# Feed-forward pieces that end with their sums: residual and second norm moved into the next token stage

## The chip, the cores and the metric

One core of a Trainium2 chip runs the whole program. A core has TensorE (PE, matmuls; its weight loads are shown apart as PEld), VectorE (DVE), ScalarE (ACT), GpSimd (POOL) and SyncE (SP), which here only issues transfers. The five run side by side. Each takes its own instructions in the order in which the program names them, and waits in front of one whose inputs or buffers are not ready. The metric is the device time of one execution in microseconds; the median of the runs stands for a kernel.

## What is computed

Four images of 64 x 64 positions and 256 channels, all in float32. A first layer adds the output of full attention over the 4096 positions. The second is triangle attention over rows with a feed-forward part and two layer norms:

```python
f, g, v = xt @ Wf + bf, xt @ Wg + bg, xt @ Wh + bh
beta = softmax(einsum('bqd,bkd->bqk', g, f))
x = x + (einsum('bqk,bkd->bqd', beta, v) @ Wo0 + bo)

q, k, v1, v2 = x @ Wq, x @ Wk, x @ Wv1, x @ Wv2          # 8 heads of 32
att = softmax(einsum('bilhd,bljhd->biljh', q, k) / sqrt(32), axis=2)
out = einsum('biljh,bilhd,bljhd->bijhd', att, v1, v2)
h = layer_norm(x + out @ Wo1) * ln_agg_g + ln_agg_b
mlp = relu(h @ W1 + b1) @ W2 + b2
return layer_norm(mlp + h) * ln_out_g + ln_out_b
```

## The kernel before

The order of all instructions is written by hand: what the Python code emits first stands first in its engine's queue. The batches go one after the other, and each has two stages.

**The token stage** (`layer0`) is the first layer. It walks through 64 groups g, eight to a query block of 512 (k = g % 8). In `values(g)` PE multiplies the exponents of group g with the values (L571) and makes the scores of group g + 1 in between (L544); ACT turns them into exponents (L556), in two halves of 1024 columns; DVE adds them up (L578). Scores have two buffers of two banks (tag "a"), exponents two (tag "k8"). From the second query block on, the eight groups also carry parts of the block before: at k = 0 the denominator (L596), its reciprocal, the product and two reductions on DVE (L600, L602, L610), at k = 1 the output (L623, and L624 on DVE), then the projections. The first query block has none of these parts.

**The triangle stage** (`first_layer1` for batch 0, `next_layer1` for the others) has 32 steps. It goes by a list of words, run through once per period of two steps; a word `R14/2` is product 4 of the period's second step, two periods late. R multiplies attention weights with v2 on DVE or POOL (L999), A accumulates the product on PE (L1009), T copies the sum out on ACT (L1019) and the second T stores it with eight transfers, S and W make weights, t and c turn them, V prepares wsel, sp and sf make scores and e and f take them. Products on DVE share three buffers (R), those on POOL two (Rp). Scores are made in 11 of the periods after the first.

Batch 1's triangle stage also carries the feed-forward of batch 0, batch 2's that of batch 1, and batch 3's that of batch 2 and the first pieces of its own. One piece of 256 positions goes with each period: h0 and h1 make x + attention output in PSUM (hps), sa takes its mean and variance, rr and pp make the scale and shift from them (Ln and Exp on ACT, seven small instructions on POOL), fa normalises into `h` (one buffer), ht turns it on PE, hT makes the input of the hidden layer from that, and hU, in `carried`, a second turned copy with the residual's scale and bias. m, r and z are the two feed-forward layers; z also turns hU's copy back into the sums in PSUM with four transposes (L1240). so takes the sums' mean and variance on ACT, and rr and pp handle them together with those of the next piece's first norm. fo normalises, and fi either finishes the piece (batch 3) or sends z off to a DRAM tile `raw` (`put_off`).

These pieces come back in the next token stage: at g = 3t `recall` fetches piece t, at g = 3t + 2 `finish` scales and shifts it on POOL (L1248, L1249) and writes it out. All of these transfers, the stores of the projections and those of the triangle stage go through SP's queue, in order.

The places that the change and the steps of the prediction touch: the list `ORDER` (L43), the calls of `recall` and `finish` in `layer0` (L752 to L755), `rest.carried` at its end (L816), `put_off` and `recall` (L1045 to L1054), `stats`, `sums_of`, `roots`, `polish`, `affine`, `carried`, `outputs` and `finish` (L1090 to L1250), and the words sa, so, rr, pp, fo, hU and fi in `next_layer1`.

Of the kernel before, what the change touches and what calls it, by code (L numbers as in the profile page):

```python
# [10 lines left out]
F32 = mybir.dt.float32  # L11
# [4 lines left out]
ALU = mybir.AluOpType  # L16
AX = mybir.AxisListType

P = 128
C = 256  # L20
# [9 lines left out]
NP = T // 256  # L30
# [10 lines left out]


ORDER = """  # L43
    r0/1 A10/2 A11/2 m1/1 R14/2 R05/1 S1/1 R15/2 T10/2 sp/1 A14/2 A16/2 r1/1 e0/1 e1/1 A15/2 A05/1 T11/2 R04/1
    A04/1 z0/1 W1/1 R03/1 V1/1 fi/2 S0 z1/1 t1/1 so/1 R06/1 R00/1 c1/1 sa A03/1 R07/1 R02/1 A06/1 A02/1 A00/1
    rr/1 pp/1 W0 R01/1 A07/1 A01/1 fo/1 fa T01/1 R12/1 t0 T00/1 R17/1 h1/-1 sf/1 R13/1 h0/-1 f0/1 ht f1/1 R16/1
# [20 lines left out]
def attention_then_triangle_kernel(  # L67
# [6 lines left out]
    nc = tc.nc  # L74
    NB = x.shape[0]
# [5 lines left out]
    work = ctx.enter_context(tc.tile_pool(name="work", bufs=2))  # L81
# [29 lines left out]
    back_t = ctile([P, 4], "back")  # L111
# [50 lines left out]
    lag_bc = brow(lag, C, "lag_bc")  # L162
# [327 lines left out]
    def layer0(b, F, safe, rest, ahead):  # L490
# [238 lines left out]
        for g in range(8 * NQB):  # L729
            qb, k = divmod(g, 8)  # L730
            if b == 0 and not safe:
                for load in later[3 * g : 3 * g + 3]:
                    load()
                if g == 6:
                    fold_bias()
                if g == 20:
                    add_b2()
            if safe and k == 0 and qb + 1 < NQB:
                mx, todo = pieces(qb + 1)
                for qc, t in todo:  # L740
                    max_piece(qc, t, mx)
                row[qb + 1] = max_row(mx)
            values(g, g + 1 < 8 * NQB)

            if qb > 0 and not (qb == last and k >= 6 + late):
                for part in parts[k]:
                    part(qb - 1)
            if late and g % 2 == 0 and 0 <= g // 2 - 2 < ahead.n:
                ahead.bring(g // 2 - 2)
            if late and g % 2 == 1 and 0 <= g // 2 - 3 < ahead.n:  # L750
                ahead.turn(g // 2 - 3)
            if b > 1 and g % 3 == 0 and g < 3 * NP:  # L752
                rest.recall(NP * (b - 2) + g // 3)
            if b > 1 and g % 3 == 2 and g < 3 * NP:
                rest.finish(NP * (b - 2) + g // 3)  # L755
            if qb == last and k == 3:
                L.fetch_v1(0)
                L.fetch_v1(1)
            if qb == last and k == 5:
                if b > 0:  # L760
                    rest.load(NP * (b - 1))
                L.fetch_qk(0, True)
# [49 lines left out]
        if old:  # L812
            rest.turn(t0)
            rest.load(t0 + 1)
            rest.normed(t0)
            rest.carried(t0)  # L816
        if not late:
            values1(1)
        score(2)
# [216 lines left out]
    class Tokens:  # L1036
        def __init__(self):
            self.ios = []
            self.A, self.htp = {}, {}
            self.h, self.hT, self.hT2, self.hid, self.z, self.zp, self.hps = {}, {}, {}, {}, {}, {}, {}  # L1040
            self.mv = self.rs = None
            self.raw = {}


        def put_off(self, tt):  # L1045
            b, t = divmod(tt, NP)
            if t == 0:
                self.raw[b] = dram.tile([NP, P, 2, C], F32, tag="raw", name="raw")
            nc.sync.dma_start(out=self.raw[b][t], in_=self.z.pop(tt))

        def recall(self, tt):
            b, t = divmod(tt, NP)
            self.z[tt] = work.tile([P, 2, C], F32, tag="s4", name="z")
            nc.sync.dma_start(out=self.z[tt], in_=self.raw[b][t])  # L1054

        def load(self, tt, far=False):
            b, t = divmod(tt, NP)
# [332 lines left out]
    def words_of(order):  # L1390
        for w in order:
            w, late = (w.split("/") + ["0"])[:2]
            yield w, int(late)
# [58 lines left out]
    def next_layer1(b, L, rest, ahead, F):  # L1452
        own = b == NB - 1
        t0 = NP * (b - 1)


        n2, n1, n0 = NP, NP + own, NP + 2 * own
        stored, held = set(), []
        mv, rs, rn, mps = {}, {}, {}, {}

        def fetched(step):
            if F is not None and 24 <= step < 31:
                ahead.fetch(F, b + 1, step)


        def load(q, far=False):
            if q < NP or 24 + (q - NP) // 2 in stored:
                rest.load(t0 + q, far)
            else:
                held.append((q, far))  # L1470

        def was_stored(step):
            stored.add(step)
            if own and step == 26:
                held.extend((NP + q, True) for q in (2, 3, 4))
            todo, held[:] = list(held), []
            for q, far in todo:
                load(q, far)

        def moments(q):  # L1480
            if q not in mv:
                mv[q] = small.tile([P, 4, 2], F32, tag="mv", name="mv")
            rest.mv = mv[q]

        def of_piece(word, q):
            tt = t0 + q
            first, second = 1 <= q < n1, 0 <= q < n2
            if word in ("h0", "h1"):
                if 2 <= q < n0:
                    n = int(word[1])  # L1490
                    rest.heads(tt, n, new=q not in mps)
                    mps.setdefault(q, {})["h", n] = True
                    if len(mps[q]) == 2 and q + 1 < n0:
                        load(q + 1)
            elif word == "sa" and first:
                moments(q - 1)
                rest.stats(rest.hps[t0 + q], 0)
            elif word == "so" and second:
                moments(q)
                z = rest.z[t0 + q] = work.tile([P, 2, C], F32, tag="s4", name="z")  # L1500
                rest.sums_of(rest.zp[t0 + q], z, rest.mv, 2)
            elif word == "rr" and second:
                moments(q)
                rest.roots(0 if q + 1 < n1 else 2, 4)
                rs[q] = rest.rs
            elif word == "pp" and second:
                moments(q)
                rest.rs = rs.pop(q)
                rest.polish(0 if q + 1 < n1 else 2, 4, nc.gpsimd, back=back_t)
                rn[q] = rest.rn  # L1510
            elif word == "fa" and first:
                rest.rn = rn[q - 1]
                rest.affine_a(tt)
            elif word == "fo" and second:
                rest.rn = rn[q]
                rest.affine_o(tt)
            elif word == "ht" and first:
                rest.turn(tt)
            elif word == "hT" and first:
                rest.normed(tt)  # L1520
            elif word == "hU" and first:
                rest.carried(tt)
            elif word in ("m0", "m1") and first:
                n = int(word[1])
                mps[q][n] = [rest.hidden(tt, fc) for fc in (2 * n, 2 * n + 1)]
            elif word in ("r0", "r1") and first:
                n = int(word[1])
                for fc, mp in zip((2 * n, 2 * n + 1), mps[q][n]):
                    rest.rectify(tt, fc, mp)
            elif word in ("z0", "z1") and second:  # L1530
                n = int(word[1])
                rest.outputs(tt, n, new=tt not in rest.zp)
                mps.setdefault(q, {})["z", n] = True
            elif word == "fi" and second:
                (rest.finish if own else rest.put_off)(tt)

        def spread(step):
            if F is not None:
                ahead.spread(F, b + 1, step)

        step_word, scores, take_scores = step_words(L, fetched, was_stored, spread)
        mps[1] = {}
        for period in range(NP + 4):
            for word, late in words_of(ORDER):
                i = period - late
                if i == 0 and word in ("A05", "A04"):
                    for m in (4, 5) if word == "A04" else ():
                        step_word("A", 0, m)
                elif word[0] in "RATSWVtc":
                    step_word(word[0], 2 * i + int(word[1]), int(word[-1]))  # L1550
                elif word in ("sp", "sf"):
                    if (i == 0) == (word == "sf"):
                        scores(i)
                elif word in ("e0", "e1", "f0", "f1"):
                    if (i == 0) == (word[0] == "f"):
                        take_scores(i, int(word[1]))
                else:
                    of_piece(word, i)
        assert not held
        if F is not None:  # L1560
            ahead.fetch(F, b + 1, NSTEP)
# [68 lines left out]
```

## Time and profile before

| | us |
|---|---|
| median of 3 runs | 3650.46 (3650.37 to 3651.98) |
| the profiled execution | 3654.27 |
| its span, first to last instruction | 3652.5 |
| token stage of batch 1 (872.4 to 1257.8) | 385.4 |
| token stages of batches 2 and 3 | 385.7, 385.6 |
| batch 1's triangle stage, first sums to the next stage's scores (1295.9 to 1744.4) | 448.5 |

Busy time of each engine over the span:

```profile
PE 3544.0 (97%) x22410; PEld 1909.6 (52%) x22410; DVE 2739.5 (75%) x2326; ACT 1934.8 (53%) x4209; POOL 1805.7 (49%) x918
```

The groups of instructions that the change touches or that its cost is taken from; the columns are busy time and mean ns of one, then the idle time of the engine before them and what ended it:

```profile
L1186 ACT ACTIVATE hT<-htp,lab_sb,lag_sb 128x256 f32<-128x256 f32 x226 | 109.6, 563 | 24.2 <-PE htp L1181 24.2
L1097 DVE BATCH_NORM_STATS2 st<-hp 128x6 f32<-128x256 f32 x128 | 52.8, 412 | 17.6 <-PE hp L1086 17.6
L1158 ACT ACTIVATE z<-zp,rn 128x256 f32<-128x256 f32 x98 | 50.0, 561 | 33.2 <-POOL rn L1153 31.5
L1098 DVE BATCH_NORM_AGGREGATE mv<-st 128x2 f32<-128x6 f32 x160 | 29.1, 182 | 8.6 <-DVE st L1097 0.5
L1124 ACT ACTIVATE ln<-mv,eps 128x4 f32<-128x4 f32 (+2 forms) x83 | 25.7, 309 | 64.4 <-DVE mv L1098 60.4 <-issue 3.5 <-DVE nt L1136 0.5
```

An engine that is idle costs nothing by itself; what counts in each stage is the one that the others wait for.

### The profile page before, as it was taken

How to read it: one execution, taken by the hardware profiler on the slowest of the kernel's cores; microseconds unless marked ns; L12 is line 12 of the kernel's file. 1: busy time of each engine (PE TensorE's matmuls, PEld its weight loads, DVE VectorE, ACT ScalarE, POOL GpSimd, SP SyncE). 2: the span in 40 equal slices, each digit the busy share in tenths (PEclk: the TensorE clock that was granted, in tenths of full speed). 3: DMA queues.
4: the chain of work that ended last, by engine and by line, in shares of the span. 5: the costliest groups of instructions: out<-in, count | busy, mean ns of one | idle time of the engine just before them, and what ended most of it. 6: DMA issues, size and time to landing. Idle time of an engine off the chain costs nothing.

```text
span 3652.5 us, 58549 instructions
## 1 busy us (share of the span) xinstructions
PE 3544.0 (97%) x22410; PEld 1909.6 (52%) x22410; DVE 2739.5 (75%) x2326; ACT 1934.8 (53%) x4209; POOL 1805.7 (49%) x918
## 2 busy tenths in 40 slices
PE   9999899988999999999999999999999999999998
PEld 6555444434555555554455555554455555555477
DVE  4777599996555479999565549999755556999976
ACT  3444455544444367666444457676544436777654
POOL 5000199994000068889311028889722106999910
PEclk9999999999999999999999999999999999999999
DMA  9544555465111343425422153333522225341221
GB/s 174 140 130 121 137 150 143 118 135 126 52 49 52 97 116 95 94 51 104 101 80 79 58 144 92 78 89 66 129 73 78 75 83 137 91 96 47 68 69 52
DMA packets 487987, 353.38 MB, mean 97 GB/s; under 512 B 302673, under 2 KB 433489, under 8 KB 478865
## 3 DMA queue, kind: packets, MB, share of 16 engines
q1 hardware_dynamic: 438656, 322.58, 33.1%
q0 software_dynamic: 36160, 19.94, 5.1%
q10 hardware_dynamic: 12880, 7.01, 0.7%
q8 instruction: 179, 2.93, 0.3%
q14 instruction: 112, 0.91, 0.1%
HBM read 197.34 MB, written 152.04 MB: 96 GB/s over the span
## 4 chain that ended last, share of the span: by engine, by line
PE 68%; POOL 5%; DVE 4%; issue 3%; ACT 2%; DMA 1%; SPq 0%; ACTq 0%; DVEq 0%; POOLq 0%
PE o L571 18%; PE acc L1009 15%; PE proj L638 6%; PE mp L1214 6%; PE zp L1234 5%; PE s L544 5%; POOL Rp L999 4%; DVE R L999 3%; PE sp L897 3%; PE hp L1081 3%; PE v1p L670 2%; PE y L623 1%; PE att L951 1%; PE htp L1181 1%; PE hp L1086 1%
## 5 line engine op out<-in xcount | busy, mean ns | idle before, releaser
L999 POOL TENSOR_TENSOR Rp<-attP,v 128x2048 f32<-128x2048 f32 x328 | 1491.1, 4576 | 463.3 <-ACT attP L959 367.8
L999 DVE TENSOR_TENSOR R<-att,v 128x2048 f32<-128x2048 f32 x696 | 1547.7, 2274 | 67.7 <-PE acc L1009 49.4
L571 PE MATMUL o<-e,v 128*128 128x512 f32 x2048 | 1043.6, 592 | 0.0
L578 DVE TENSOR_TENSOR esum<-esum,e 128x2048 f32<-128x2048 f32 x224 | 525.0, 2344 | 508.9 <-ACT e L556 505.6
L556 ACT ACTIVATE e<-s 128x1024 f32<-128x1024 f32 x512 | 523.4, 1024 | 581.3 <-PE s L544 484.6
L544 PE MATMUL s<-gT,fT 128*128 128x512 f32 x1024 | 785.6, 769 | 8.6 <-ACT e L556 5.1
L1009 PE MATMUL acc<-R,wsel 128*32 128x512 f32 x5568 | 705.7, 602 | 37.2 <-DVE R L999 29.4
L571 PEld LDWEIGHTS o<-e,v 128*128 128x128 f32 x2048 | 388.7, 190 | 275.9 <-issue 233.6
L1009 PE MATMUL acc<-Rp,wsel 128*32 128x512 f32 x2624 | 344.3, 596 | 11.1 <-POOL Rp L999 10.4
L1019 ACT COPY ao<-acc 128x1024 f32<-128x1024 f32 x256 | 254.4, 1021 | 189.6 <-PE acc L1009 153.1
L1009 PEld LDWEIGHTS acc<-R,wsel 128*32 128x32 f32 x5568 | 152.1, 109 | 384.5 <-issue 277.9
L544 PEld LDWEIGHTS s<-gT,fT 128*128 128x128 f32 x1024 | 194.2, 190 | 243.9 <-issue 231.0
L1142 POOL TENSOR_SCALAR nt<-mv 128x4 f32<-128x4 f32 (+1 forms) x51 | 9.8, 192 | 627.2 <-DVE mv L1098 623.1
L1248 POOL TENSOR_TENSOR z<-z,log_bc 128x512 f32<-128x512 f32 x48 | 71.8, 1496 | 452.2 <-DMA z<-raw 434.5
L934 ACT ACTIVATE es<-S,rd 128x64 f32<-128x64 f32 x1024 | 257.8, 336 | 16.6 <-DVE rd L926 13.8
L1214 PE MATMUL mp<-hT,w 128*128 128x256 f32 x1024 | 249.5, 389 | 0.7 <-ACT hT L1186 0.7
L1234 PE MATMUL zp<-w,hid 128*128 128x256 f32 x1024 | 245.0, 385 | 0.8 <-ACT hid L1223 0.8
L1214 PEld LDWEIGHTS mp<-hT,w 128*128 128x128 f32 x1024 | 186.8, 190 | 101.2 <-ACT attP L959 36.0
L1234 PEld LDWEIGHTS zp<-w,hid 128*128 128x128 f32 x1024 | 185.7, 190 | 62.3 <-issue 29.3
L600 DVE RECIPROCAL rec<-den 128x512 f32<-128x512 f32 x32 | 107.4, 3358 | 119.4 <-PE den L596 114.0
L1009 PEld LDWEIGHTS acc<-Rp,wsel 128*32 128x32 f32 x2624 | 81.5, 110 | 197.8 <-issue 139.0
L1223 ACT ACTIVATE hid<-mp,b_sb 128x256 f32<-128x256 f32 x256 | 105.2, 469 | 117.7 <-PE mp L1214 117.7
(180 smaller groups left out, 3665.7 us busy)
## 6 DMA issues: line engine op xcount, KB each, us to landing
v<-v2d SPq DMA_DIRECT2D x44, 512.0 KB
v1c<-v1d SPq DMA_DIRECT2D x128, 128.0 KB
aT<-ao SPq DMA_DIRECT2D x1024, 16.0 KB
A<-aT SPq DMA_DIRECT2D x256, 64.0 KB
out_dram<-z SPq DMA_DIRECT2D x63, 256.0 KB
y<-yT SPq DMA_DIRECT2D x56, 256.0 KB
q<-st SPq DMA_DIRECT2D x56, 256.0 KB
k<-st SPq DMA_DIRECT2D x52, 256.0 KB
```

The lines of the kernel that those rows point to most:

```text
L544: nc.tensor.matmul(s_ps[r // 2][:, r % 2, :], fT[tt][:, ts(r * 4 + n, P)], gT[qb // 4][:, ts(qb % 4, QB)], start=True, stop=not safe,)
L556: nc.scalar.activation(e[g][:, 2 * j : 2 * j + 2, :], s_ps[j], AF.Exp)
L571: nc.tensor.matmul(o_ps[qb], F.v[tt][:, r * 4 + n, :], es[:, r, :], start=(k == 0 and r == 0), stop=(k == 7 and r == 3),)
L578: nc.vector.tensor_tensor(esum[qb], esum[qb], es, ALU.add)
L638: nc.tensor.matmul(ps, w[:, cc, rows], y(qb, cc), start=(cc == 0), stop=(cc == 1))
L897: nc.tensor.matmul(sp[ts(h, 64), lh, n, :], k[rows, u * 8 + n, :], q[rows, u * 8 + n, :], start=True, stop=True,)
L934: nc.scalar.mul(e[:, i, :], rows[:, i, :], rec[:, i : i + 1])
L999: eng.tensor_tensor(R, src.unsqueeze(1).to_broadcast([P, D, N]), v2[h], ALU.mult)
L1009: nc.tensor.matmul(acc[32 * c : 32 * c + 32, n % 2, :], w[:, n, c, 16 * h : 16 * h + 32], R[:, ts(c, 8), :].rearrange("p d j -> p (d j)"), ...
L1019: nc.scalar.copy(self.ao[step][:, ts(np, 2)].rearrange("p k d j -> p k (d j)"), self.acc[step][np])
L1214: nc.tensor.matmul(self.mp[:, fc % 2, :], w1_sb[:, cc, ts(fc, P)], self.hT[tt][:, cc, :], start=(cc == 0), stop=(cc == 1),)
L1234: nc.tensor.matmul(zp[:, n, :], self.hid[tt][:, fc, ts(n, P)], w2_sb[:, fc, :], start=(fc == 0), stop=(fc == 3 and tt not in self.hT2),)
```

## The change

For batches 0 and 1 (the pieces that go with the triangle stages of batches 1 and 2) the piece ends with the sums of the second feed-forward layer. so becomes a plain copy out of PSUM, fi sends that copy off, and hU sends off `h` as fa left it, with no second turned copy and so without the four transposes back. rr and pp handle the first norm alone, and sa takes its sums on ACT (`sums_of`) where DVE took them. The DRAM tile `raw` holds both halves of a piece, 0.5 MB.

In the next token stage `recall` fetches both into a tile of tag R. At g = 3t + 2 `settle` makes the residual on DVE (h times its scale, plus its bias, added to z), takes the statistics on DVE and Ln and Exp of them on ACT. At g = 3t + 3, ahead of the next `recall`, `conclude` does the small instructions of the norm on DVE, the two normalising activations on ACT and `finish` on POOL. Batch 3's triangle stage keeps the old order as `ORDER_LAST`; the two others go by a new list.

```diff
 ORDER = """
+    R17/2 A10/2 A12/2 R13/2 fo/2 f1/2 ht/1 h1 hT/1 t0/1 m0/1 A13/2 R14/2 A11/2 R15/2 R02/1 f0/2 R16/2 W1/1 c0/1
+    A17/2 r0/1 T10/2 A14/2 R05/1 A16/2 V0/1 A15/2 sp/1 T11/2 R03/1 m1/1 h0 t1/1 A02/1 e0/1 R01/1 e1/1 S0 c1/1
+    r1/1 sa A03/1 A05/1 fi/2 V1/1 R07/1 R00/1 R06/1 S1 A01/1 z1/1 W0 R04/1 rr/1 z0/1 hU/1 R10/1 A00/1 A07/1
+    A06/1 pp/1 R12/1 T00/1 A04/1 so/1 fa T01/1 sf/1 R11/1
+""".split()
+ORDER_LAST = """
...
+            if b > 1 and g % 3 == 0 and 0 < g <= 3 * NP:
+                rest.conclude(NP * (b - 2) + g // 3 - 1)
             if b > 1 and g % 3 == 0 and g < 3 * NP:
                 rest.recall(NP * (b - 2) + g // 3)
             if b > 1 and g % 3 == 2 and g < 3 * NP:
-                rest.finish(NP * (b - 2) + g // 3)
+                rest.settle(NP * (b - 2) + g // 3)
...
-            rest.carried(t0)
+            (rest.carried if b == NB - 1 else rest.carried_off)(t0)
...
+        def carried_off(self, tt):
+            self.put_off(tt, 0, self.h.pop(tt))
+
+        def summed_off(self, tt):
+            self.put_off(tt, 1, self.z.pop(tt))
 
         def recall(self, tt):
             b, t = divmod(tt, NP)
-            self.z[tt] = work.tile([P, 2, C], F32, tag="s4", name="z")
-            nc.sync.dma_start(out=self.z[tt], in_=self.raw[b][t])
+            self.both[tt] = work.tile([P, 2, 2, C], F32, tag="R", name="hz", bufs=3)
+            nc.sync.dma_start(out=self.both[tt], in_=self.raw[b][t])
+
+        def settle(self, tt):
+            both = self.both.pop(tt)
+            h, z = both[:, 0], both[:, 1]
+            nc.vector.tensor_tensor(h, h, lag_bc.unsqueeze(1).to_broadcast([P, 2, C]), ALU.mult)
+            nc.vector.tensor_tensor(h, h, lb2_bc.unsqueeze(1).to_broadcast([P, 2, C]), ALU.add)
+            nc.vector.tensor_tensor(z, z, h, ALU.add)
+            self.z[tt] = z
+            self.stats(z, 2)
+            self.roots(2, 4)
+            self.settled[tt] = self.mv, self.rs
+            self.mv = None
+
+        def conclude(self, tt):
+            self.mv, self.rs = self.settled.pop(tt)
+            self.polish(2, 4, nc.vector)
+            self.affine(self.z[tt], self.z[tt], 2)
+            self.finish(tt)
...
             elif word == "sa" and first:
                 moments(q - 1)
-                rest.stats(rest.hps[t0 + q], 0)
+                if own:
+                    rest.stats(rest.hps[tt], 0)
+                else:
+                    junk = work.tile([P, 2, C], F32, tag="sx", name="junk", bufs=1)
+                    rest.sums_of(rest.hps[tt], junk, rest.mv, 0)
             elif word == "so" and second:
+                z = rest.z[tt] = work.tile([P, 2, C], F32, tag="s4", name="z")
+                if own:
+                    moments(q)
+                    rest.sums_of(rest.zp[tt], z, rest.mv, 2)
+                else:
+                    nc.scalar.copy(z, rest.zp.pop(tt))
...
-            elif word == "fo" and second:
+            elif word == "fo" and second and own:
...
-                rest.carried(tt)
+                (rest.carried if own else rest.carried_off)(tt)
...
-                (rest.finish if own else rest.put_off)(tt)
+                (rest.finish if own else rest.summed_off)(tt)
```

More of the change, by code (lines that the diff above doesn't have):

```diff
@@ L1041, in __init__, with put_off @@
             self.mv = self.rs = None
-            self.raw = {}
-        def put_off(self, tt):
+            self.raw, self.both, self.settled = {}, {}, {}
+        def put_off(self, tt, part, src):
             b, t = divmod(tt, NP)
-            if t == 0:
-                self.raw[b] = dram.tile([NP, P, 2, C], F32, tag="raw", name="raw")
-            nc.sync.dma_start(out=self.raw[b][t], in_=self.z.pop(tt))
+            if b not in self.raw:
+                self.raw[b] = dram.tile([NP, P, 2, 2, C], F32, tag="raw", name="raw")
+            nc.sync.dma_start(out=self.raw[b][t][:, part], in_=src)
+        def carried_off(self, tt):
+            self.put_off(tt, 0, self.h.pop(tt))
+        def summed_off(self, tt):
+            self.put_off(tt, 1, self.z.pop(tt))
         def recall(self, tt):
             b, t = divmod(tt, NP)
-            self.z[tt] = work.tile([P, 2, C], F32, tag="s4", name="z")
-            nc.sync.dma_start(out=self.z[tt], in_=self.raw[b][t])
+            self.both[tt] = work.tile([P, 2, 2, C], F32, tag="R", name="hz", bufs=3)
[16 more added lines that the diff above has]
+            self.finish(tt)
         def load(self, tt, far=False):
@@ L1496, in of_piece @@
                 moments(q - 1)
-                rest.stats(rest.hps[t0 + q], 0)
-            elif word == "so" and second:
-                moments(q)
[L1500 to L1504, printed above, removed]
+                if own:
[3 more added lines that the diff above has]
+                    rest.sums_of(rest.hps[tt], junk, rest.mv, 0)
+            elif word == "so" and second:
+                z = rest.z[tt] = work.tile([P, 2, C], F32, tag="s4", name="z")
[4 more added lines that the diff above has]
+                    nc.scalar.copy(z, rest.zp.pop(tt))
+            elif word == "rr" and second and (own or q + 1 < n1):
+                moments(q)
+                rest.roots(0 if q + 1 < n1 else 2, 4 if own else 2)
                 rs[q] = rest.rs
-            elif word == "pp" and second:
+            elif word == "pp" and second and (own or q + 1 < n1):
                 moments(q)
                 rest.rs = rs.pop(q)
-                rest.polish(0 if q + 1 < n1 else 2, 4, nc.gpsimd, back=back_t)
+                if own:
+                    rest.polish(0 if q + 1 < n1 else 2, 4, nc.gpsimd, back=back_t)
+                else:
+                    rest.polish(0, 2, nc.gpsimd, back=back_t[:, 2:4])
                 rn[q] = rest.rn
@@ L1543, in next_layer1 @@
         for period in range(NP + 4):
-            for word, late in words_of(ORDER):
+            for word, late in words_of(ORDER_LAST if own else ORDER):
                 i = period - late
-                if i == 0 and word in ("A05", "A04"):
+                if own and i == 0 and word in ("A05", "A04"):
                     for m in (4, 5) if word == "A04" else ():
```

## The prediction

> **What bounds the kernel now.** I read the cores view first (one core, granted clock 0.994, so no clock story), then the busy times by stretch, cut at the stage borders that the score matmuls (L544) and the triangle products (L999) show. The stretches below are three triangle periods of batch 1 and the two token stages before and after that triangle stage; the columns are length, then busy time and instructions of PE, PEld, DVE, ACT, POOL, then clock and DMA.
>
> ```profile
> 1383.70:1411.50 27.80, 27.80 (x256) 14.96 (x252) 26.91 (x21) 19.64 (x54) 24.13 (x13) 1.00 0.54 124
> 1660.40:1687.40 27.00, 26.18 (x188) 12.79 (x184) 26.79 (x20) 17.52 (x52) 26.41 (x16) 1.00 0.58 88
> 1714.30:1743.30 29.00, 23.50 (x184) 9.49 (x176) 27.31 (x15) 11.92 (x32) 26.78 (x18) 1.00 0.41 76
> 872.40:1257.80 385.40, 383.59 (x1077) 202.91 (x1074) 203.49 (x135) 162.19 (x183) 0.00 (x0) 1.00 0.19 59
> 1744.40:2130.10 385.70, 383.92 (x1077) 202.88 (x1074) 212.60 (x133) 162.49 (x183) 62.16 (x33) 1.00 0.28 80
> ```
>
> See three regimes. A triangle period that still makes scores is 27.80 us long, PE fills all of it, DVE 26.91. In the last periods there are no scores, and DVE (26.79 of 27.00) and POOL (26.41) set the pace. A token stage is PE alone; the one that finishes old pieces on POOL (62 us) is only 0.3 us longer than the one that does not.
>
> The chain of waits inside one triangle period names the PE work that the change takes out:
>
> ```profile
> 1392.68 1.93 PE zp L1234 x8
> 1394.61 0.22 PE zp L1240 x2
> 1394.83 1.73 PE zp L1234 x8
> 1396.55 0.22 PE zp L1240 x2
> ```
>
> **Triangle stages of batches 1 and 2, per piece (one piece a period).** PE loses the four L1240 transposes: 0.22 + 0.22 = 0.44 us. DVE loses two bn_stats and two bn_aggr of hps: 2 x 0.412 + 2 x 0.182 = 1.19 us. ACT takes these sums and drops the same four activations on zp, drops hU (2 x 0.563) and fo (2 x 0.561) and gains one copy (0.58, from the 128x512 copy L650): 1.67 us less of 19.64. POOL keeps its seven polish instructions. SP gets one more issue (0.58, from the row of L1049); it is queued behind the eight stores of T11, the next piece's loads and V1's fetch, and fa of the next period waits for its landing since h has one buffer.
>
> Periods with scores: 27.80 - 0.44 = 27.36 us, DVE then 25.7, still under it. The word sp runs in 11 periods: 4.8 us. The three scoreless ones are held by POOL, which the change leaves alone (26.41 of 27.00): between 0 and 1.2 us each, I take 0.4 because the POOL row is that near, 1.2 in all. The last 29 us have no bn_stats: 0. At the end of the token stages before these triangle stages, the piece's two hU activations give way to one transfer, off PE's chain: 0. The first period I give 1 us (bounds -3 to +3, the DVE waits of 3.9 and 3.2 us there being what another order could lose or win). Sum 7 us per stage, 14 for both. The new order itself: I added up its words on PE, and every product has its DVE or POOL result before its turn, the tightest being hT before m0 (some 0.1 us) and the h transfer before fa (some 2 us). In periods that also fetch 2 MB (v2, q, k) that transfer may be late; bounds 0 to 3 us in five such periods, 0 to 15 per stage; I take 0, as the 0.25 MB recall below lands in 3 us in ordinary traffic.
>
> **Token stages of batches 2 and 3.** Added per piece, on DVE in settle: multiply, add, add (0.685, 0.692, 0.685 from L1205, L1206 and L1106) and 1.19 of statistics, 3.25 us; in conclude four polish instructions of 0.16 (L1136 to L1139), 0.64 us. On ACT: Ln and Exp (0.309 + 0.205 = 0.51) in settle, two affines (2 x 0.56 = 1.12) in conclude. POOL as before. DMA: 0.5 MB come back instead of 0.25. By busy time it is 16 x 3.9 = 62 us on DVE, which has 173 free: nothing. But engines take instructions in the order of the program, and Ln stands on ACT in front of the next group's exponents. If the statistics are late, the exponents are late, and a score matmul needs the buffer that the first exponent of the group before reads (two s buffers). On DVE the next esum stands behind settle, and the exponent two groups on waits for that esum (two e buffers, 3.04 us of it below); on SP the recall and the stores of projections stand behind the output of the piece before. One such place, at the turn of a query block (group k=0, then k=1):
>
> ```profile
> 1838.57 3.36 DVE L600 RECIPROCAL rec<-den 128x512 f32<-128x512 f32 x1 [5.10 <-PE den L596]
> 1841.96 0.69 DVE L602 TENSOR_TENSOR oT<-o,rec 128x512 f32<-128x512 f32 x1
> 1843.17 0.68 DVE L610 TENSOR_REDUCE dens<-esum 128x1 f32<-128x512 f32 x1
> 1843.76 2.28 DVE L578 TENSOR_TENSOR esum<-esum,e 128x2048 f32<-128x2048 f32 x1
> 1845.96 1.40 DVE L624 SCALAR_TENSOR_TENSOR yT<-y,bo_sb,yT 128x512 f32<-128x512 f32 x2
> ...
> 1839.89 1.02 ACT L556 ACTIVATE e<-s 128x1024 f32<-128x1024 f32 x1 [1.62 <-PE s L544]
> 1846.13 1.02 ACT L556 ACTIVATE e<-s 128x1024 f32<-128x1024 f32 x1 [3.04 <-DVE esum L578]
> ...
> 1844.13 0.79 PE L544 MATMUL s<-gT,fT 128*128 128x512 f32 x1
> ```
>
> The reader is to see DVE without a gap from 1838.57 to 1847.36 (the second reduction of L610 stands between), an exponent at 1839.89, and the score at 1844.13 which must not start before that exponent ends: 3.2 us of slack. Settle at k=0 (groups 8 and 32) starts on DVE at 1843.85: 1843.85 + 3.25 = 1847.10, Ln and Exp 1847.61, exponent 1848.63; PE waits 4.5. Conclude at k=0 (groups 24 and 48): 1843.85 + 0.64 + 1.12 + 1.02 = 1846.63, PE waits 2.5. Settle at k=1 (17 and 41) starts after L624: 1847.36 + 3.25 + 0.51 + 1.02 = 1852.14 against the next block's opening at 1850.19, PE waits 1.95. Twice each: 17.9 us.
>
> At k=2 to 7 the block is 6.1 to 7.8 us long, DVE idles 3.4 to 5.5 of it, and the slack covers settle as long as the transfer is there. That is what the second pair of places hangs on:
>
> ```profile
> 1766.72 0.41 SPq L1054 DMA_DIRECT2D z<-raw  x1
> 1769.68 1.28 POOL L1248 TENSOR_TENSOR z<-z,log_bc 128x512 f32<-128x512 f32 x1 [3.48 <-DMA z<-raw]
> 1771.04 3.20 POOL L1249 TENSOR_TENSOR z<-z,lob_bc 128x512 f32<-128x512 f32 x1
> ```
>
> A recall of 0.25 MB takes 3.0 us to be used; twice the bytes between 3.0 and 6.0, I take 4. And in the new order recall(t+1) stands on SP behind the output of piece t, which waits for polish, affine and POOL's 2.6 to 4.5 us. In the blocks of 6 us that puts the data some 4 us after settle could start, and ACT is free again about 2 us before PE would wait. In the first query block a group lasts only 4.35 us (no projections). Group 2: the first recall is used at 1762.3 today, behind 3 MB of loads; 1763.3 + 3.25 + 0.51 + 1.02 = 1768.1 against a block opening at 1765.0: 3.1. Group 5, by the same chain through SP: 2.9. Bounds for each 0 to 8. So a token stage pays 17.9 + 6.0 = 23.9 us, from 14 (half the slack misjudged) to 34; two stages 48.
>
> DMA: Bandwidth & Descriptors, in Anatomy of one DMA, gives 2.0 us and the bytes at 436 GB/s for one transfer (fitted there on the GpSimd path), an estimate of 2.6 us for the old recall and 3.2 for the new one, so the Trainium skill would have the new one only 0.6 us later; the old one's 3.0 us here is near it. By it group 5 pays 2.5 and the total drops by under 1 us. The skill's Perfetto Trace Analysis, Identifying the Most-Contended Engine, takes occupancy as the fair measure for Vector and Scalar; by that rule the token stages, at 55% and 42%, take the added work free and the sum would be -14 us; the rows of 1838 to 1847 speak against it, since a mean over the stage hides stretches in which DVE has no gap.
>
> **Sum.** Against the profiled execution's span of 3652.5 in its 3654.3 us: 3654.3 - 14 + 48 = 3688. The runs' median of 3650.46 is 3.8 lower: **3684**.
>
> **Rivals.** (a) Faster: PE has enough prepared work to ride over the ACT waits, so the token stages stay at 385.7 as they did when POOL's finish came in (0.3 us). Mechanism: Ln waits only as long as DVE lags, place the token stages, price 0 to 2 a stage: 3650.5 - 14 + 4 = 3640. For it: nothing waits there now, ACT is 42% busy. Against: 3.2 us of slack at 1844.13 and 7.7 us asked of it. It decides once the token stages pay under 7 us each. (b) Smaller loss: only the k=0 settles bite and the transfers are early, 2 x 9 to 2 x 13 = about 22: 3650.5 - 14 + 22 = 3658. (c) The change does not do what it says in the triangle: the h transfer holds fa, 3 us in five periods, 15 a stage eats the 7: 3684 + 30 = 3714. For it: one h buffer and SP's eight stores of 0.6 us each; against: some 2 us of room in ordinary periods.
>
> **Chances.** Forecast 0.63 (own range 3664 to 3706), (a) 0.12, (b) 0.15, (c) 0.10. About 0.2% (7 us) is what a measurement can tell from no change. (a) splits into 0.10 faster and 0.02 same, (b) into 0.03 same and 0.12 slower, the rest is slower: 0.10, 0.05, 0.85. The range leaves out most of (a) and half of (c): 3652 to 3712.
>
> **What would show it.** Token stages of batches 2 and 3 about 24 us longer than 385.7 while batch 1's stays 385.4; PE waiting for e (L556) at eight places a stage, 4.5 us at groups 8 and 32; Ln on ACT waiting for mv before it; the first triangle periods 27.3 to 27.4 instead of 27.8. Wrong if a token stage stays under 393, if a period is not shorter, or if h (L1158) waits for raw.

## The result, and the profile after

| | before | after |
|---|---|---|
| median | 3651.22 us (3650.37 to 3652.03) | 3803.01 us (3798.28 to 3806.26) |
| runs | 4 | 4 |
| span of the profiled execution | 3652.5 | 3804.5 |
| mean granted clock of PE | 0.994 | 0.976 |
| token stages of batches 2 and 3 | 385.7, 385.6 | 413.2, 410.6 |
| triangle stages of batches 1 and 2 | 486.5, 486.6 | 536.7, 538.1 |

The ratio is 1.0415, with a 95% interval of 1.0397 to 1.0433: slower by 152 us, where the prediction said 34. A triangle stage is counted here from the end of one token stage's last score to the next one's first. The extra 152 us of span are 52.5 in the two token stages (+27.5 and +25.0; +23.9 each was predicted) and 101.7 in the two triangle stages (+50.2 and +51.5; -7 each was predicted), less some 2 us elsewhere. All other stages are as they were.

From the profile after: the busy time of each engine over the span, then groups of instructions with the columns as before (busy, mean ns of one, idle time before them and what ended it).

```profile
PE 3578.3 (94%) x22282; PEld 1933.9 (51%) x22282; DVE 2825.8 (74%) x2558; ACT 1928.4 (51%) x4221; POOL 1784.9 (47%) x904
```
```profile
L1220 ACT ACTIVATE hT<-htp,lab_sb,lag_sb 128x256 f32<-128x256 f32 x162 | 80.6, 561 | 39.6 <-PE htp L1215 39.3
L969 ACT COPY attP<-att 128x192 f32<-128x192 f32 (+1 forms) x128 | 38.3, 299 | 310.9 <-DVE R L1009 242.4 <-PE att L961 68.5
L1158 ACT ACTIVATE ln<-mv,eps 128x2 f32<-128x2 f32 (+2 forms) x113 | 33.5, 297 | 161.4 <-DVE mv L1132 156.6 <-issue 4.3 <-DVE nt L1170 0.5
L1131 DVE BATCH_NORM_STATS2 st<-hp 128x6 f32<-128x256 f32 x68 | 28.1, 414 | 17.5 <-PE hp L1120 17.5
L1131 DVE BATCH_NORM_STATS2 st<-hz 128x6 f32<-128x256 f32 x64 | 26.3, 411 | 1.1
```

The reader sees that what was to go did go: 128 fewer transposes and matmuls on PE (22410 to 22282), 64 fewer turned copies on ACT (226 to 162 of hT's line), and the statistics split between hp and hz. PE is nevertheless busy for 34 us longer, with fewer instructions. And ACT waits 242 us (62 before) for DVE's products in front of a copy, attP, that the diff does not touch, except for where it stands.

The busy time by stretch has the same columns as before (length; PE, PEld, DVE, ACT, POOL; clock; DMA). Of after: batch 1's triangle stage, an ordinary period of it, one in which v2 is fetched too, and the two token stages.

```profile
1257.10:1793.80 536.70, 484.06 (x4049) 260.75 (x4048) 428.47 (x253) 295.42 (x820) 395.47 (x208) 0.95 0.42 96
1562.80:1593.50 30.70, 28.34 (x250) 15.68 (x249) 25.95 (x16) 18.21 (x52) 23.99 (x13) 0.94 0.28 64
1526.50:1562.80 36.30, 29.68 (x246) 16.46 (x246) 26.11 (x16) 16.88 (x50) 22.70 (x12) 0.88 0.63 145
1793.80:2207.00 413.20, 393.09 (x1077) 205.14 (x1074) 267.71 (x309) 182.60 (x247) 53.56 (x32) 0.98 0.29 85
2745.00:3155.70 410.70, 391.56 (x1077) 204.03 (x1074) 268.16 (x309) 182.42 (x246) 53.59 (x32) 0.99 0.28 85
```

A period that was 27.80 us with PE full is now 30.70 with 2.4 us of idle PE, at a clock of 0.94. No engine is full in it: the period is set by a chain that crosses engines. A fetch period is 36.30.

**Where a triangle period loses it.** The timeline of after, around the loss in one period (start, length, engine, line, instruction; in brackets the idle time before it and what ended it):

```profile
1487.36 2.28 DVE L1009 TENSOR_TENSOR R<-att,v 128x2048 f32<-128x2048 f32 x1
1489.67 0.32 ACT L969 COPY attP<-att 128x192 f32<-128x192 f32 x1 [5.91 <-DVE R L1009]
1489.89 0.84 ACT L1257 ACTIVATE hid<-mp,b_sb 128x256 f32<-128x256 f32 x2
1490.61 1.02 ACT L1029 COPY ao<-acc 128x1024 f32<-128x1024 f32 x1
1491.69 1.98 PE L907 MATMUL sp<-q,k 32*64 32x64 f32 x64 [2.36 <-ACT ao L1029]
1493.60 3.32 PE L1248 MATMUL mp<-hT,w 128*128 128x256 f32 x8
```

Read it from below. The scores sp wait 2.36 us for the copy ao (word T10), which frees their buffer in PSUM. ao stands on ACT behind hid (r0), and that behind attP (c0). attP begins 0.03 us after a product R on DVE ends, and ACT has stood idle for 5.91 us in front of it. That product is R02/1, which the new list puts ahead of c0/1. It reads att, the tile in PSUM that attP copies. The two share nothing else, so it seems that the build makes the later of two reads of one PSUM tile by different engines wait for the earlier; experiment 1 tests it. R02 in turn stands in DVE's queue behind R13, R14 and R15. So one word in front of c0 has tied ACT's queue to the end of DVE's. The waits by instruction of after in this stage (us in total, times, longest) give the sums of that chain:

```profile
ACT attP L969 <- DVE R L1009: 91.6, 15, 8.0
POOL Rp L1009 <- ACT attP L969: 80.2, 13, 18.3
DVE R L1009 <- PE acc L1019: 65.9, 20, 6.8
PE sp L907 <- ACT ao L1029: 25.8, 11, 2.4
ACT h L1192 <- DMA raw<-h: 12.4, 2, 6.4
```

Eleven waits of PE come to 25.8 us, one in each period with scores. The last line is a second, rarer wait: fa, which makes the next h, waits for the transfer of the h before, in two fetch periods.

**The clock.** The last line of the timeline shows another thing: mp takes 3.32 us where eight matmuls of it take 1.89 at other places of this stage. The same place one period later, by microseconds (the third number from the end is the granted clock):

```profile
1521.00:1522.00 1.00, 0.00 (x0) 0.00 (x0) 1.00 (x1) 1.00 (x3) 1.00 (x1) 1.00 0.00 0
1523.00:1524.00 1.00, 1.00 (x44) 1.00 (x40) 1.00 (x2) 0.98 (x3) 1.00 (x1) 0.81 0.00 0
1524.00:1525.00 1.00, 1.00 (x18) 0.78 (x11) 1.00 (x1) 0.82 (x2) 1.00 (x1) 0.50 0.50 114
1526.00:1527.00 1.00, 1.00 (x3) 0.80 (x3) 0.53 (x1) 0.43 (x1) 1.00 (x1) 0.50 0.71 197
1527.00:1528.00 1.00, 1.00 (x6) 0.84 (x5) 0.35 (x2) 0.00 (x0) 1.00 (x1) 0.98 1.01 229
```

PE was idle from 1520.07 to 1522.43; from 1523.6 to 1527.0 it runs at half its clock. Each of these eleven waits is paid for twice, first as idle time and then as slow work.

**Where a token stage loses it.** The timeline of after at group 8, a place that the prediction worked through with the rows of 1838 to 1847 (a few microseconds later here):

```profile
1843.60 3.36 DVE L608 RECIPROCAL rec<-den 128x512 f32<-128x512 f32 x1 [0.27 <-PE den L604]
1848.19 0.68 DVE L618 TENSOR_REDUCE dens<-esum 128x1 f32<-128x512 f32 x1
1848.78 0.68 DVE L1075 TENSOR_TENSOR hz<-hz,lag_bc 128x512 f32<-128x512 f32 x1
...
1851.94 0.18 DVE L1132 BATCH_NORM_AGGREGATE mv<-st 128x2 f32<-128x6 f32 x1
1852.04 2.26 DVE L586 TENSOR_TENSOR esum<-esum,e 128x2048 f32<-128x2048 f32 x1
1852.16 0.29 ACT L1158 ACTIVATE ln<-mv,eps 128x2 f32<-128x2 f32 x1 [8.86 <-DVE mv L1132]
1852.49 0.20 ACT L1160 ACTIVATE rs<-ln 128x2 f32<-128x2 f32 x1
1852.60 1.92 ACT L564 ACTIVATE e<-s 128x1024 f32<-128x1024 f32 x2
1853.66 0.50 PE L552 MATMUL s<-gT,fT 128*128 128x512 f32 x1 [3.94 <-ACT e L564]
```

It is the chain that was forecast: DVE without a gap, settle from 1848.78 to 1852.12, ACT idle 8.86 us in front of Ln while two exponents stand behind it, and PE waits 3.94 us for the exponent.

### The profile page after: what moved, and what is told of

Its sections match the earlier page's. It is cut to its first block, busy times and chain, and to the rows that moved or that the text cites. A ratio compares the mean times of both kernels' runs of the same rounds, so it can differ in the third digit from the quotient of the medians.

```text
span 3804.5 us, 58498 instructions
## 1 busy us (share of the span) xinstructions
PE 3578.3 (94%) x22282; PEld 1933.9 (51%) x22282; DVE 2825.8 (74%) x2558; ACT 1928.4 (51%) x4221; POOL 1784.9 (47%) x904
## 4 chain that ended last, share of the span: by engine, by line
PE 55%; DVE 10%; POOL 7%; issue 6%; ACT 3%; DMA 2%; SPq 1%; ACTq 0%; DVEq 0%; POOLq 0%
PE o L579 14%; PE acc L1019 11%; PE proj L646 6%; POOL Rp L1009 6%; DVE R L1009 5%; PE mp L1248 5%; PE zp L1268 5%; PE s L552 4%; PE sp L907 2%; PE v1p L678 2%; PE hp L1115 2%; DVE rec L608 1%; DMA hz<-raw 1%; PE att L961 1%; ACT ao L1029 1%
## 5 line engine op out<-in xcount | busy, mean ns | idle before, releaser
L1019 PE MATMUL acc<-R,wsel 128*32 128x512 f32 x5568 | 701.8, 604 | 30.7 <-DVE R L1009 23.9
L1282 POOL TENSOR_TENSOR hz<-hz,log_bc 128x512 f32<-128x512 f32 x32 | 55.4, 1733 | 561.6 <-ACT hz L1192 561.6
L1176 POOL TENSOR_SCALAR nt<-mv 128x2 f32<-128x2 f32 (+1 forms) x49 | 9.5, 193 | 591.1 <-DVE mv L1132 587.2
L1248 PE MATMUL mp<-hT,w 128*128 128x256 f32 x1024 | 277.0, 421 | 5.4 <-ACT hid L1257 4.3
L1248 PEld LDWEIGHTS mp<-hT,w 128*128 128x128 f32 x1024 | 208.7, 212 | 74.4 <-ACT hid L1257 23.0
L969 ACT COPY attP<-att 128x192 f32<-128x192 f32 (+1 forms) x128 | 38.3, 299 | 310.9 <-DVE R L1009 242.4
```

What stands on the lines that cost most here:

```text
L1019: nc.tensor.matmul(acc[32 * c : 32 * c + 32, n % 2, :], w[:, n, c, 16 * h : 16 * h + 32], R[:, ts(c, 8), :].rearrange("p d j -> p (d j)"), ...
L1248: nc.tensor.matmul(self.mp[:, fc % 2, :], w1_sb[:, cc, ts(fc, P)], self.hT[tt][:, cc, :], start=(cc == 0), stop=(cc == 1),)
```

## The experiments

Three edits each undo one suspected cost by moving the same work to another place. They were made alone, then together; what each changes of the code is shown. The three alone have two runs each, and the length of a stage is from one profiled execution of each kernel. Nothing of the computation is left out in any of them.

**1. The product R02 behind the copy c0.** Only the place of one word changes, in the new list:

```diff
-    ... A11/2 R15/2 R02/1 f0/2 R16/2 W1/1 c0/1
+    ... A11/2 R15/2 f0/2 R16/2 W1/1 c0/1 R02/1
```

> One word moves: R02/1 stands behind c0/1 in the new list. Theory A (the copy c0 of the turned weights waits for product R02, which reads the same PSUM tile and stands ahead of it; r0, T10 and so sp wait behind c0 on ACT): the triangle periods fall from 30.7-32 us to 27.4-27.8, those that wait for the h transfer (36) to 30-32, each triangle stage is 35 to 45 us shorter, the whole about 3715 to 3730; token stages stay at 411 to 413. Rival B (the h transfer on SP's queue holds fa): at most 5 us a stage, over 3785. Rival C (three R buffers are too few for the new list, DVE waits for PE): periods stay over 30, over 3780.

Measured: 3712.5 us (3707.85 to 3717.15), ratio to the kernel before 1.0167 (1.0130 to 1.0204). The triangle stages are 490.5 and 491.1 us, 46 and 47 less than in the changed kernel. The token stages stay at 413.4 and 410.3. The waits of this kernel in batch 1's triangle stage:

```profile
ACT attP L969 <- PE att L961: 25.2, 16, 2.5
ACT h L1192 <- DMA raw<-h: 22.6, 6, 7.9
```

No attP waits for DVE any more, only for the transposes that write att, and the row of sp waiting for ao is gone. Ordinary periods are 27.0 us. Two fetch periods a stage remain, at 34.7 and 34.2 from scores to scores, and the wait of h for its transfer has grown from 12.4 to 22.6 us. One word was worth 46 us a stage.

**2. The transfer of h started earlier.** hU, which sends h off, goes from behind z0 to right behind hT; in the profiles h is sent off some 17 us earlier:

```diff
-    ... ht/1 h1 hT/1 t0/1 m0/1 ...
+    ... ht/1 h1 hT/1 hU/1 t0/1 m0/1 ...
...
-    ... rr/1 z0/1 hU/1 R10/1 A00/1 A07/1
+    ... rr/1 z0/1 R10/1 A00/1 A07/1
```

> One word moves: hU/1 stands right behind hT/1, so that h is sent off some 15 us earlier, ahead of the stores and loads on SP's queue. Theory A: only the periods of 36 us change, to 31 to 32; 6 to 15 us a stage, the whole 3775 to 3795. Rival B (the h transfer is the main cause): all periods to 27.5 to 28.5, about 3715. Rival C: no change, 3803.

Measured: 3777.85 us (3774.43 to 3781.27), ratio 1.0346 (1.0315 to 1.0377). The triangle stages are 522.8 and 524.4, 14 less than in the changed kernel. From scores to scores the two fetch periods of batch 1's stage fall from 37.6 us to 30.8 and 30.7, and the others with scores are as they were, within 0.2. So the transfer does hold fa, in two periods a stage, and c0 holds all the others.

**3. Root, small instructions and activations later in the token stage.** settle keeps its place at g = 3t + 2, but ends with the statistics. The rest goes to later groups:

```diff
+                if g % 3 == 0:
+                    if 1 <= t <= NP:
+                        rest.rooted(first + t - 1)
+                    if t < NP:
+                        rest.recall(first + t)
+                    if 2 <= t <= NP + 1:
+                        rest.finish(first + t - 2)
+                elif g % 3 == 1:
+                    if 1 <= t <= NP:
+                        rest.polished(first + t - 1)
+                else:
+                    if 1 <= t <= NP:
+                        rest.concluded(first + t - 1)
+                    if t < NP:
+                        rest.settle(first + t)
...
+        def rooted(self, tt):
+            self.mv = self.settled[tt]
+            self.roots(2, 4)
```

polished holds the four small instructions, concluded the two activations. Ln then stands on ACT a group behind the statistics, and each next step a group or more behind the one before.

> The new list as it is. In the token stages Ln and Exp are emitted one group after the statistics, the four small DVE instructions two groups after, the affines three, POOL's finish four, behind the next recall. Theory (ACT's queue stands still in front of Ln or the affine, the next exponents come late, PE waits for them, 2 to 4.5 us at eight places): each token stage of batches 2 and 3 falls from 411-413 to 386-392 us, the whole to 3755 to 3765; triangle stages stay at 537. Rival (the added DVE time or the 0.5 MB recall itself costs PE the time): the token stages stay over 404, the whole over 3790.

Measured: 3754.32 us (3752.59 to 3756.05), ratio 1.0282 (1.0252 to 1.0311). The token stages fall from 413.2 and 410.6 to 389.6 and 388.1, the triangle stages stay at 536.4 and 535.4. The whole token stage of batch 2 by busy time, in this kernel:

```profile
1792.10:2181.70 389.60, 384.61 (x1077) 202.60 (x1074) 268.21 (x309) 183.47 (x246) 50.03 (x32) 1.00 0.30 90
```

The same instructions with the same busy time on DVE (268.2 against 267.7) and ACT (183.5 against 182.6) cost 24 us less. The work was never too much; it stood in the wrong place of two queues.

**4. The three together.**

> All three edits. If the causes are these and add up: triangle periods with scores at 27.36 us (27.80 in the kernel before, less the four transposes), token stages at 386 to 392, the whole 3635 to 3655. If something else of the new list holds PE (R buffers, POOL), periods stay over 28 and the whole over 3665.

Measured: 3636.49 us (3632.87 to 3638.19), ratio 0.9963 (0.9944 to 0.9983): faster than the kernel before. Token stages 389.2 and 388.7, triangle stages 474.7 and 475.4. The three gains add up: in the first of each pair of stages 46.2 (edit 1), 15.8 more by edit 2, and 24.0 by edit 3.

**5. The old list with the new pieces.** Is the shorter triangle stage due to the work that was taken out, or to the new order? Here edit 3 stands, and the triangle stages of batches 1 and 2 go by the old list:

```diff
-            words_of(ORDER_LAST if own else ORDER)
+            words_of(ORDER_LAST)
```

> The pieces end with their sums as in the change, with Ln, Exp, affines and finish spread as in the run that did so; but the triangle stages of batches 1 and 2 go by the list of the kernel before (its fo word does nothing). It tells what the new list is worth by itself. If the triangle period follows PE's work alone: 27.80 - 0.44 = 27.36 us and tails no shorter, triangle stages 478 to 482, the whole 3640 to 3648. If the old list's own waits keep the period: 27.8, 486, the whole 3656. If it reaches 27.0 as the new list did, the new list brings nothing and the whole is 3634 to 3640.

Measured: 3645.38 us (3643.74 to 3648.3, ten runs), ratio 0.9979 (0.9970 to 0.9989), on another chip than the four before. Triangle stages 480.1 and 480.3. An ordinary period of this kernel:

```profile
1440.00:1467.30 27.30, 27.30 (x250) 14.54 (x249) 25.84 (x16) 18.42 (x52) 24.02 (x13) 1.00 0.23 61
```

PE fills the period, which is 27.30 us long; 27.80 - 0.44 = 27.36 was predicted. The stage is 6.5 us shorter than before. The new order, once mended, gives another 3 to 5 us a stage: over a triangle stage PE is busy for 461.9 and 463.5 us in experiment 7's kernel, which has the mended order, and for 468.2 and 466.6 here, with the same number of instructions.

**6. Still later in the token stage.** As experiment 4, with Ln and Exp one group later again, the small instructions three groups behind settle, and the activations with the finish four behind it, next to the recall.

> All three edits, with Ln and Exp one group later still (two after the statistics), the small DVE instructions three after, affines and finish four. By the queue theory the last 3 to 4 us of each token stage (1.2 us at groups 10 and 34, 0.5 to 1.6 at group 4: Ln waits for the statistics that follow the turn of a query block) go as well: token stages 385.7 to 386.5, the whole 6 us shorter than with the three edits alone, 3628 to 3633. If those waits are of the transfer or of DVE: 3634 to 3640.

Measured: 3648.2 us (3645.64 to 3653.17), ratio 0.9987 (0.9978 to 0.9996): this expectation failed. Token stages 396.4 and 393.3, worse than 389. The timeline of this kernel at group 8:

```profile
1781.31 0.15 DVE L1188 SCALAR_TENSOR_TENSOR nt<-mv,rs 128x2 f32<-128x2 f32 x1
...
1781.96 0.69 DVE L1085 TENSOR_TENSOR hz<-hz,lag_bc 128x512 f32<-128x512 f32 x1
...
1783.26 1.28 POOL L1300 TENSOR_TENSOR hz<-hz,log_bc 128x512 f32<-128x512 f32 x1 [10.05 <-ACT hz L1210]
1783.41 1.67 DVE L1087 TENSOR_TENSOR hz<-hz 128x512 f32<-128x512 f32 x1
...
1786.20 2.26 DVE L586 TENSOR_TENSOR esum<-esum,e 128x2048 f32<-128x2048 f32 x1
1788.38 1.40 DVE L632 SCALAR_TENSOR_TENSOR yT<-y,bo_sb,yT 128x512 f32<-128x512 f32 x2
...
1789.17 3.68 PE L646 MATMUL proj<-yT,wq 128*128 128x512 f32 x4 [2.58 <-DVE yT L632]
```

Ln no longer delays anything here, but settle still stands at the turn of a query block, ahead of esum and yT, on a DVE that has no gap there. PE waits for yT, which the next projection reads, 2.58 us at each of the two turns with a settle in batch 2's stage; behind each of these waits the granted clock is 0.50 for 3.4 us. In experiment 4's kernel the same wait is 0.95. The 1.63 us more are the four small instructions, which now stand right ahead of settle (0.65), and the addition of hz, which takes 1.67 us beside the finish on POOL where it takes 0.69 alone. What had to move, it seemed, was settle itself, away from the turn; experiment 7 tests it.

**7. Settle kept off the turn of a query block.** The three edits, but with the pieces at chosen groups, none in k = 0 or 1 with its settle (the two activations of the pieces at 5, 13 and 21 do fall on k = 0, at groups 8, 16 and 24, although the expectation below says that none does):

```diff
+                starts = (3, 5, 10, 12, 13, 18, 20, 21, 26, 28, 34, 36, 42, 44, 50, 52)
+                for t, at in enumerate(starts):
+                    if g == at - 2:
+                        rest.recall(first + t)
...
+                    if g == at + 1:
+                        rest.rooted(first + t)
+                    if g == at + 2:
+                        rest.polished(first + t)
+                    if g == at + 3:
+                        rest.concluded(first + t)
+                        rest.finish(first + t)
+                    if g == at:
+                        rest.settle(first + t)
```

> The first three edits together, but the pieces no longer go at every third group. Each settle stands at group 2, 4 or 5 of a query block (in the first block at 3 and 5), the root one group later, the small instructions two, the affines and the finish three, the fetch two groups before. So no settle and no affine stands in the two groups at a query block's turn, where DVE has no gap. Theory (the token stage pays only where added work meets the turn of a query block in an in-order queue): token stages of batches 2 and 3 386 to 387.5 (389 with a settle at every third group), triangle stages 474 to 476 as before, the whole 3628 to 3634, some 4 us under the next run. Rival (what is left is DMA traffic or DVE's total load): token stages stay at 388 to 390.

Beside it ran experiment 4's kernel once more, on the same chip:

> The three edits together once more, for a comparison on the same chip: 3632 to 3638, token stages of batches 2 and 3 389, triangle stages 475. Ratio to the kernel before 0.995 to 0.997.

Measured: 3631.64 us (3628.97 to 3632.88), ratio 0.9942 (0.9928 to 0.9956), and for the repeat 3636.93 us (3632.8 to 3639.53), ratio 0.9959 (0.9945 to 0.9972). The busy time by stretch of the first: batch 1's triangle stage and the two token stages.

```profile
1255.60:1730.40 474.80, 461.92 (x4048) 244.86 (x4046) 426.67 (x253) 297.25 (x820) 395.72 (x208) 1.00 0.47 108
1730.40:2116.40 386.00, 384.12 (x1077) 202.63 (x1074) 272.83 (x309) 183.31 (x246) 43.17 (x33) 1.00 0.31 91
2593.20:2979.20 386.00, 384.12 (x1077) 202.69 (x1074) 272.75 (x309) 183.34 (x247) 42.80 (x32) 1.00 0.30 91
```

The token stages are 386.0 us, within 0.4 of those before, with 60 us more work on DVE than they had, and 3 us below those of the repeat (389.3 and 388.9). The three pairs of activations at k = 0 cost nothing that can be seen; in the profile ACT waits in front of none of them. This is the fastest version of the study, 21 us under the kernel before.

## Why the prediction was wrong

**The token stage was right, in its mechanism and nearly in its sum** (23.9 predicted, 27.5 and 25.0 measured). By place, the lengthening of the group's block against that of the kernel before, in batch 2's and batch 3's stage:

| place | predicted | measured |
|---|---|---|
| settle at k = 0 (groups 8, 32) | 4.5 each | 4.2, 4.5; 4.5, 4.2 |
| conclude at k = 0 (24, 48) | 2.5 each | 2.2, 2.2; 2.2, 2.2 |
| settle at k = 1 (17, 41) | 1.95 each | 1.7, 1.6; 1.7, 1.7 |
| group 2 | 3.1 | 3.9; 2.4 |
| group 5 | 2.9 | 0; 0.4 |
| settle at k = 2 (26) | 0 | 0.7; 0.7 |
| the next block after groups 2, 8 and 32 | 0 | 2.5, 1.7, 2.4; 1.7, 1.7, 1.7 |

Two terms were off, in opposite directions, so that the sum is closer than its parts. Group 5's 2.9 is hardly there. And the blocks behind the three longest waits are long as well, a term that the sum did not have: of batch 2's 27.5 us, 9.2 are PE working at the lower clock (busy 393.1 us for what took 383.9 before), and only 18.3 are more idle time. Rivals (a) and (b) fall with this. Experiment 3 shows the cause, since moving Ln and what follows it gives 23.6 and 22.5 us back with the busy times of DVE and ACT unchanged.

**The triangle stage's saving was right.** The period of 27.36 us came out at 27.30 with the old list (experiment 5), and the stage at -6.5 against -7.

**The step that failed** is this one: "The new order itself: I added up its words on PE, and every product has its DVE or POOL result before its turn". It checks whether PE's inputs arrive, product by product, and takes for granted that every other engine starts its words when its own inputs are there. It does not ask what each word on ACT has to wait for in the new order. c0 there waits for R02, one for each of the 15 waits counted above; c0 holds r0 and T10, T10 holds the scores. Put at 0, this cost 46 us a stage (experiment 1). The profile of before held the row that should have prompted the question. These are the waits of the kernel before in batch 0's triangle stage, which goes by a list of its own that neither kernel changes:

```profile
ACT attP L959 <- DVE R L999: 61.8, 16, 8.0
```

Sixteen waits of ACT's copy for DVE's product, though both only read att. In batches 1 to 3 there was none of them, because the old list had its R words for the same att behind c0. The Trainium skill's page PSUM — Partial Sum Buffer, in PSUM bank collisions raise a hardware error, says that the compiler puts a dependency between any two instructions on different engines that touch the same bank and quadrant of partitions, reads included and ScalarE against VectorE too. The trace agrees with the dependency (15 waits, 91.6 us in the changed kernel, all gone in experiment 1, where the two words change places); whether an access without it would fail was not tried.

**The transfer of h was a bound taken at the wrong end.** The prediction gave "0 to 15 per stage; I take 0". Experiment 2 measures 14 in the changed kernel, and from experiment 1 to experiment 4 it is 15.8 in the first stage. Rival (c) named the place and the price, but it came as two waits of 7 us, not five of 3. Its reason for 0, a recall that lands in 3 us in ordinary traffic, was no evidence for the periods that were in question, since those fetch 2 MB as well.

**The clock was not considered**, because it was 0.994 before. But a forecast that adds waits to PE has to ask what they do to it. Over batch 1's triangle stage PE's busy time is 484.1 us in the changed kernel and 461.9 in experiment 7, with the same instructions: 22 of the 62 us between them are slower work, 40 are idle time (52.6 against 12.9).

Together, for batch 1's stage, going back from the changed kernel's 536.7 us: -46.2 (c0), -15.7 (the transfer of h, experiment 1 to 7) gives 474.8, which is 11.7 under the kernel before; 6.5 of that is the work taken out and the rest the order.

Why PE is busy for less time in the new order stays open. It may be that PE changes less often between kinds of matmul there; no run tells this apart from other causes.

## What to carry to other kernels

When an order written by hand changes, go through every engine's queue, not only that of the engine that sets the pace: for each word, what does it wait for now that stands earlier, and who stands behind it? Two reads of one PSUM tile by two engines count as such a wait. Put a step that waits on another engine at least one stage of work behind what it waits for, and keep added work out of the stretches where its engine has no gap; busy time alone said nothing here (268 us of DVE work cost 27 us in one order, 273 us cost 0.3 in another).

## What the runs showed of the hardware

**Waits of PE of 2.3 us were followed by half its clock.** In batch 1's triangle stage of the changed kernel PE was idle for more than 1 us 23 times. With all 14 idle times of 2.31 to 4.31 us the clock went to 0.50, for 3.4 us, or 6.8 with the two longest; after all 9 of 1.23 to 1.87 us it stayed at 1.00. The next token stage adds two of 1.94 us that left it at 1.00. Of one of these, by microseconds (PE idle from 1958.88 to 1960.83):

```profile
1959.00:1960.00 1.00, 0.00 (x0) 0.00 (x0) 1.00 (x1) 1.00 (x3) 0.06 (x1) 1.00 0.00 0
1961.00:1962.00 1.00, 1.00 (x4) 0.50 (x4) 1.00 (x2) 0.69 (x1) 1.00 (x1) 1.00 0.06 16
1963.00:1964.00 1.00, 1.00 (x5) 0.57 (x3) 1.00 (x1) 0.49 (x1) 1.00 (x1) 1.00 0.00 0
```

The page TensorE: Matmul & The Clock Gate of the Trainium skill, in Part 1: The HAM clock gate, has the gate fall back to half after an idle window of about 3.4 us. By that the eleven waits of 2.31 to 2.36 us in this stage should have cost nothing beyond themselves; the trace shows the half clock after each of them. Such a wait costs another 1.4 us (3.3 us for mp instead of 1.9). The length of a wait does not decide alone, and no limit can be read from these runs: in the same trace the clock stayed at 1.00 after a wait of 2.55 us (412.37 to 414.93) and was 0.50 for 3.4 us after one of 1.83 us (678.55 to 680.38). What else decides stays open.

**DVE can slow down beside POOL.** At the place shown in experiment 6, the addition of hz on DVE takes 1.67 us beside POOL's finish, against a mean of 0.69 us in the changed kernel. It does not always: in experiment 4's kernel settle's multiplication takes 0.69 us beside POOL's addition (at 1835.11), and the addition right behind it, beside the same instruction of POOL, 1.64. What makes the difference was not tried.
